# Last batch's rows: plain loads and 0/1 products in place of indexed gathers, and the mean's share added ahead

## The chip, the core and the metric

The kernel runs on one core of a Trainium2 chip. The metric is device time in microseconds, the median of several runs. The core has five engines with a queue of instructions each, worked off in order: PE (TensorE, with its weight loads shown as PEld), DVE (VectorE), ACT (ScalarE), POOL (GpSimd) and SP (SyncE, which here issues transfers and little else). ACT, POOL and SP issue DMA transfers, and 16 DMA engines carry them out. A queue whose head waits holds all that is behind it.

## The reference

Masked attention over 8 batches of 512 features x 1024 tokens, plus the input. One projection serves as queries, keys and values:

```python
q = xt @ Wq.T                       # xt: (B, T, D), 8 heads of 64
scores = scale * jnp.einsum('bhqd,bhkd->bhqk', qh, qh)
logits = (scores * cmask + (1.0 - cmask) * NEG) * rmask
attn = jax.nn.softmax(logits, axis=-1)
ctx = jnp.einsum('bhqk,bhkd->bhqd', attn, qh)
out = ctx @ Wo.T
return x + jnp.transpose(out, (0, 2, 1))
```

The mask has ones for about half of the tokens. A token with mask 0 has all its logits 0, so its attention is the same for every key and its context is the mean of all values: all such tokens of a batch get one and the same output row, called the mean's share here.

## The kernel before

Only the kept tokens (mask 1) go through attention: each batch's are packed into NK = 536 columns (a longer version and a general one follow in the program for inputs that don't fit, and are not run). The packed tokens form NC = 5 chunks, four of 128 and a short one (index 4, LAST) of 24. Eight heads are worked in four pairs per batch. One loop in `late` runs over the 32 pairs and, in each, over five chunks: scores of the chunk (PE), exponentials with their row sums (ACT), and the weighing of values (PE, `av`), with tasks between them. Which task is issued at which (batch, pair, chunk) and in which rank within it stands in a table that `plan` fills with `put`. The position in that table is the position in each engine's queue. `weigh_behind` gives its first matmul a wait on a named instruction, the last one that read the tile it overwrites; for the last chunks that is "partials", the copy of a partial output.

Tiles carry batch and pair or chunk in their names: `pa_7_3` is the partial output of batch 7 (the last), chunk 3. For an ordinary batch the projected rows go to DRAM (`od`), each to the place that `places` gives it, and indexed gathers by POOL (`fetch`, with addition) bring one row per token to `g`, which already holds the input; DVE transposes it (`finish_blocks`) and `store_whole` writes it out, the eight pieces by turns on SP and ACT.

The last batch is different, so that little is left after its last pair. `begin_outputs` multiplies the contexts of pairs 0 to 2 by the output weights during pair 3 and copies the partial sums out of PSUM on ACT (`pa`). After the last chunk come the sums and their inverses (`sum_last`, `inverses`), whose reciprocals PE spreads over partitions (`rb`, L828) and ACT copies (L835), then `end_values_last` (cT), and `end_outputs` adds pair 3's product (`po`) to `pa` on DVE (`oc`, three buffers) and stores the rows to `od_7`. The last packed row holds the mean's share, and tokens with mask 0 point to it. Then `fetch_last` gathers, for each of eight tiles of 128 tokens, the rows named by `origin`, on POOL; `finish_tokens` turns each tile by four PE transposes, DVE adds them to the input in `residual`, and SP and ACT store by turns.

## Time and profile before

| | us |
|---|---|
| runs | 726.7, 728.66, 724.15 (median 726.7) |
| the profiled execution | 730.38 |
| its span | 728.6 |
| PE busy in the span | 642.4 (88%) |
| end of the last weighing's `rb` matmuls (PE) | 694.12 |
| ACT's copy of it (L835) begins | 696.14 |
| `po` begins on PE | 698.18 |
| last rows of `od_7` issued | 706.48 |
| last gather issued on POOL | 715.67 |
| last addition on DVE begins | 722.58 |
| last store issued (ACT) | 723.30 |

The profile's times run from the span's start. A row of the timeline has the start, the length, the engine, the line, the operation with its tiles, and in brackets the idle time before it and what ended that. "ACTq" and "SPq" are those engines' transfer issues. A row of the chain of waits has start, length and what the end waited for at that time. The granted clock is the share of full TensorE speed.

### The profile page before, as it was taken

The page shows a single profiled execution, that of the slowest core. Times are in us where ns is not written, and L with a number is a line of the kernel's source. Part 1 is how long each engine was busy: PE and PEld are TensorE (multiplying, and loading weights), DVE is VectorE, ACT ScalarE, POOL GpSimd, SP SyncE. Part 2 cuts the span into 40 slices and gives each one's busy share as a digit, 9 for nine tenths or more (in the row PEclk, how much of TensorE's full clock was granted, in tenths as well). Part 3 has the DMA queues.
Part 4 walks back from the last instruction along what each step waited for, and adds up shares of the span by engine and source line. Part 5 has one row for each costly group of instructions (what it writes and reads, how often), then busy time and mean ns, then how long its engine had stood idle before and what let it go on. Part 6 is the DMA issues. An engine that isn't in the chain of part 4 may idle for free.

```text
span 728.6 us, 24594 instructions
## 1 busy us (share of the span) xinstructions
PE 642.4 (88%) x10533; PEld 419.8 (58%) x10533; DVE 403.1 (55%) x1137; ACT 322.1 (44%) x874; POOL 208.5 (29%) x228
## 2 busy tenths in 40 slices
PE   6887875899889998899889998899998999998854
PEld 5654453577556675567556675567654677554323
DVE  5578286674564775476664665576531553254333
ACT  4463542555435553356425453255443555445200
POOL 2324204000241403441241402532232411343412
PEclk9999898999999999999999998899998999999975
DMA  8787443253346956778557956665436626769867
GB/s 238 225 259 204 131 121 113 79 153 90 100 129 184 206 125 186 196 196 195 154 162 209 196 134 183 182 167 118 118 93 162 136 64 181 209 140 302 135 179 214
DMA packets 78310, 119.60 MB, mean 164 GB/s; under 512 B 13736, under 2 KB 46976, under 8 KB 78064
## 3 DMA queue, kind: packets, MB, share of 16 engines
q1 hardware_dynamic: 44448, 66.73, 31.2%
q0 software_dynamic: 15936, 35.41, 21.8%
q10 hardware_dynamic: 17808, 15.81, 8.5%
q8 instruction: 84, 1.38, 0.8%
q14 instruction: 34, 0.28, 0.1%
HBM read 74.29 MB, written 42.57 MB: 160 GB/s over the span
## 4 chain that ended last, share of the span: by engine, by line
PE 77%; issue 5%; DVE 5%; ACT 2%; another core or an unknown queue 2%; DMA 1%; ACTq 1%; POOL 0%; POOLq 0%; DVEq 0%
PE av L778 20%; PE s L731 18%; PE pq L590 15%; PE po L906 12%; PE v L369 3%; PE po L981 3%; PE s L745 2%; PE pa L981 2%; PE x L369 1%; PE pq L602 1%; DVE xbar L476 1%; PE x L922 1%; DMA g<-od,origin 1%; DVE len L681 1%
## 5 line engine op out<-in xcount | busy, mean ns | idle before, releaser
L754 ACT ACTIVATE e<-s,bias 128x536 f32<-128x536 f32 x256 | 179.1, 705 | 82.1 <-PE s L731 75.7
L731 PE MATMUL s<-qT 64*64 64x268 f32 x2048 | 179.1, 404 | 17.4 <-issue 15.6
L778 PE MATMUL av<-e,v 64*64 64x268 f32 x2048 | 165.7, 408 | 15.5 <-ACT qT L614 7.5
L731 PEld LDWEIGHTS s<-qT 64*64 64x64 f32 x2048 | 93.5, 138 | 75.2 <-issue 42.5
L590 PE MATMUL pq<-xc,wqT 64*64 64x269 f32 (+1 forms) x896 | 117.9, 397 | 1.1 <-DVE sums L842 0.9
L590 PE MATMUL pq<-xc,crossT 64*64 64x269 f32 (+1 forms) x896 | 113.6, 398 | 0.0
L778 PEld LDWEIGHTS av<-e,v 64*64 64x64 f32 x2048 | 80.6, 139 | 53.4 <-ACT cT L810 11.4
L648 DVE COPY v<-v 128x512 f32<-128x512 f32 x32 | 22.1, 692 | 144.6 <-PE v L369 144.6
L1064 POOL DMA_INDIRECT g<-od,block_origin x56 | 88.8, 1585 | 39.3 <-DMA g<-xd 16.3
L906 PE MATMUL po<-woT,cT 64*64 64x256 f32 x1536 | 98.1, 380 | 1.2 <-issue 1.0
L936 POOL DMA_DIRECT2D od<-oc x28 | 16.9, 603 | 252.0 <-ACT oc L959 226.1
L525 POOL DMA_INDIRECT xin<-xd,source x63 | 61.7, 979 | 92.5 <-DVE source L513 55.8
L906 PEld LDWEIGHTS po<-woT,cT 64*64 64x64 f32 x1536 | 65.1, 134 | 25.2 <-DVE v L663 8.1
L590 PEld LDWEIGHTS pq<-xc,wqT 64*64 64x64 f32 x896 | 66.3, 138 | 18.0 <-DVE sums L842 1.4
L590 PEld LDWEIGHTS pq<-xc,crossT 64*64 64x64 f32 x896 | 65.4, 138 | 15.9 <-issue 0.8
L754 ACT ACTIVATION_READ_ACCUMULATOR e<-s,bias 128x1 f32 x256 | 50.7, 198 | 0.0
L663 DVE COPY v<-x 128x128 f32<-128x128 f32 x32 | 9.2, 289 | 74.9 <-PE x L369 33.0
L810 ACT COPY cT<-av 128x536 f32<-128x536 f32 x31 | 18.8, 606 | 71.6 <-PE av L778 50.1
L614 ACT COPY qT<-pq 128x536 f32<-128x536 f32 x31 | 18.8, 606 | 71.4 <-PE pq L590 30.2
L754 ACT ACTIVATE el<-s,bias 128x268 f32<-128x268 f32 x64 | 30.5, 482 | 44.6 <-PE s L745 44.6
L1038 DVE STREAM_TRANSPOSE whole<-g 128x512 f32<-128x512 f32 x56 | 40.0, 750 | 12.5 <-DMA g<-od,block_origin 12.5
L498 DVE TENSOR_SCALAR_CACHE_REDUCE junk<-rank,place 128x1024 f32<-128x1024 f32 (+4 forms) x35 | 39.1, 1116 | 0.5 <-DMA rank<-ranks 0.5
(186 smaller groups left out, 770.9 us busy)
## 6 DMA issues: line engine op xcount, KB each, us to landing
xd<-xt SPq DMA_DIRECT2D x28, 512.0 KB
g<-xd SPq DMA_DIRECT2D x56, 256.0 KB
x<-in_x_dram SPq DMA_DIRECT2D x40, 256.0 KB
rb<-row SPq DMA_DIRECT2D x60, 160.0 KB
od<-oc POOLq DMA_DIRECT2D x28, 256.0 KB
out_dram<-whole SPq DMA_DIRECT2D x28, 256.0 KB
out_dram<-whole ACTq DMA_DIRECT2D x28, 256.0 KB
x<-in_x_dram ACTq DMA_DIRECT2D x24, 256.0 KB
```

Of the source, the lines that this page charges most:

```text
L369: nc.tensor.matmul(to, block, ident[heads[r], heads[r]], start=True, stop=True)
L498: nc.vector.tensor_scalar(junk[:, : T - at], rank[:, at:], place[:, col], 0.0, ALU.is_le, ALU.add, accum_out=found[:, col])
L525: nc.gpsimd.indirect_dma_start(out=to, out_offset=None, in_=of, in_offset=bass.IndirectOffsetOnAxis(ap=at, axis=0),)
L590: nc.tensor.matmul(pq[heads[c], r, :n], w[heads[r], k // 2, pr * P + c * DK : pr * P + (c + 1) * DK], xcs[b][heads[r], k, :n], start=(k == 0),
L648: copy = nc.vector.tensor_copy(v[:, :LAST, :].rearrange("p c (h d) -> p h c d", h=2), pt[:, :, :E].rearrange("p h (c d) -> p h c d", c=LAST),)
L731: nc.tensor.matmul(s[h][to, hf, :KH], qT[heads[h], at : at + DK], qT[heads[h], hf * KH : (hf + 1) * KH], start=True, stop=True,)
L754: act = nc.scalar.activation(e[:, h], of[h], AF.Exp, bias=biases[pair][:, c : c + 1], scale=SCALE, accum_out=acc[:, h, c : c + 1],)
L778: mm = nc.tensor.matmul(avs[pair][heads[h], hf, :KH], v[rows, c, heads[h]], e[rows, h, hf, :] if c < LAST else e[rows, h, :], start=(c == ...
L906: mm = nc.tensor.matmul(po[heads[c], eb, :E], cTs[b, pr][heads[r], i * P + c * DK : i * P + (c + 1) * DK], woT[heads[r], pr, eb * E : (eb ...
L981: nc.tensor.matmul(po[j * n : (j + 1) * n, :w], cTs[b, pr][:, at : at + n], woT[:, pr, j * w : (j + 1) * w], start=(pr == first), stop=(pr ...
L1038: nc.vector.transpose(in_blocks(wholes[b], b)[:, i].rearrange("p (k h) t -> p k h t", h=2), parted(gs.pop((b, i))),)
L1064: nc.gpsimd.indirect_dma_start(out=gs[b, i], out_offset=None, in_=ods[b], in_offset=bass.IndirectOffsetOnAxis(ap=block_origin[:, b, i : i ...
```

## The change

Six things change, all of them in the last batch except the second half of the fifth.

1. The rows of batch 7 are written in plain rank order, so that those that a tile of 128 tokens needs stand together. `load_begins` reads on SP, from `last_begin`, the row at which each tile starts into registers (seven loads), and `fetch_last` loads 128 rows from there by plain transfers on SP. POOL's eight gathers are gone, as are the load and copy of `origin`. `clear_outputs` zeroes the rows past the kept ones ahead.
2. `finish_tokens` no longer transposes by the identity but multiplies by a 0/1 matrix (`hot_last`) per tile, which puts the row of each kept token to its column and gives the others zero. `place_spots`, `load_spots` and `find_spots` make these matrices in earlier chunks. The PSUM tags of the eight tiles go round three names in place of two.
3. The mean's share is added ahead: `mean_output` projects it (16 short matmuls), DVE copies it, and SP sends it to DRAM and back (`spread_mean`) as rows on all partitions (`mean_wide`) and as a column (`mean_col`). `add_mean` adds the column to the whole `residual`, eight operations on POOL.
4. So the kept tokens must not get it twice: the copy of the partial outputs becomes a subtraction of `mean_wide` on DVE, no longer a copy on ACT.
5. The four short stores of `od_7_4` go to SP in place of ACT. The output stores of batches 6 and on go to SP alone; batch 5 and earlier still alternate.
6. `keep_mean` of the last pair is called in chunk 0, not 1.

On **DVE** at the end of the last pair, before (L1038 are the transposes of batch 6, L842 to L849 the sums and their reciprocals):

```order
L1038 STREAM_TRANSPOSE whole_6_8851<-g_6_4_8637 128x16x32
L1038 STREAM_TRANSPOSE whole_6_8851<-g_6_5_8716 128x16x32
L1038 STREAM_TRANSPOSE whole_6_8851<-g_6_6_8718 128x16x32
L1038 STREAM_TRANSPOSE whole_6_8851<-g_6_7_8763 128x16x32
L842 TENSOR_TENSOR sums_1_88<-sums_1_88,share_7_3_8751 128x10
L845 TENSOR_TENSOR low_85<-low_85,sums_1_88 128x8
L846 TENSOR_SCALAR sums_1_88<-sums_1_88 128x2x4
L848 RECIPROCAL ris_1_90<-sums_1_88 128x2x4
L849 COPY ris_1_90<-sums_1_88 128x2
```

and after, where L1093 are the transposes and L847 to L854 the sums:

```order
L1063 TENSOR_TENSOR pa_7_1_9003<-pa_7_1_8996,mean_wide_8888 128x512
L1063 TENSOR_TENSOR pa_7_2_9005<-pa_7_1_8996,mean_wide_8888 128x512
L1093 STREAM_TRANSPOSE whole_6_8925<-g_6_4_8681 128x16x32
L1093 STREAM_TRANSPOSE whole_6_8925<-g_6_5_8760 128x16x32
L1063 TENSOR_TENSOR pa_7_3_9029<-pa_7_3_9025,mean_wide_8888 128x512
L1093 STREAM_TRANSPOSE whole_6_8925<-g_6_6_8762 128x16x32
L1093 STREAM_TRANSPOSE whole_6_8925<-g_6_7_8807 128x16x32
L847 TENSOR_TENSOR sums_1_90<-sums_1_90,share_7_3_8795 128x10
L850 TENSOR_TENSOR low_87<-low_87,sums_1_90 128x8
L851 TENSOR_SCALAR sums_1_90<-sums_1_90 128x2x4
L853 RECIPROCAL ris_1_92<-sums_1_90 128x2x4
L854 COPY ris_1_92<-sums_1_90 128x2
```

The subtractions stand between the transposes, and the last two transposes and the sums now stand behind that of chunk 3.

On **ACT** at the same place, before (L1008 the copies of partial outputs, L1045 the stores of batch 6):

```order
L1008 COPY pa_7_1_8929<-pa_7_1_8922 128x512
L1008 COPY pa_7_2_8931<-pa_7_1_8922 128x512
L754 ACTIVATE el_7_3_4_8935,sums_1_88<-s_7_3_4_8936,bias_7_3_8749 128x268 x2
L1008 COPY pa_7_3_8955<-pa_7_3_8951 128x512
L1045 DMA out_0_dram<-whole_6_8851 32x8x256 x4
L835 COPY rb_7_3_8980<-rb_3_8981 128x128
L836 COPY rb_7_3_8980<-rb_3_8981 128x512
L936 DMA od_7_9015<-oc_7_0_9013 128x512
L946 DMA od_7_9015<-oc_7_4_9017 24x4x32 x4
```

and after:

```order
L759 ACTIVATE e_7_3_3_8975,sums_1_90<-s_7_3_3_1_8977,bias_7_3_8793 128x536
L759 ACTIVATE el_7_3_4_9009,sums_1_90<-s_7_3_4_9010,bias_7_3_8793 128x268 x2
L840 COPY rb_7_3_9062<-rb_3_9063 128x128
L841 COPY rb_7_3_9062<-rb_3_9063 128x512
L953 DMA od_7_8068<-oc_7_0_9095 128x512
L953 DMA od_7_8068<-oc_7_1_9104 128x512
```

The copies and the stores of batch 6 are gone from ahead of the copy of `rb`.

On **SP** from batch 6's last input rows on, before:

```order
L1032 DMA g_6_7_8763<-xd_6_101 128x512
L1045 DMA out_0_dram<-whole_5_8500 32x8x256 x4
L1045 DMA out_0_dram<-whole_6_8851 32x8x256 x4
L1660 TENSOR_LOAD flag_62
L1660 ISA x2
```

and after (L1032, L1040 and L1047 carry the mean, L1101 are the stores of batches 5 and 6, L963 the short stores of `od_7_4`, L1144 the first of the eight row loads):

```order
L1087 DMA g_6_7_8807<-xd_6_103 128x512
L1101 DMA out_0_dram<-whole_5_8544 32x8x256 x2
L1032 DMA means_of_81<-mean_8864 1x128 x4
L1040 DMA mean_wide_8888<-means_of_81 128x512
L1047 DMA mean_col_8890<-means_of_81 32x4x1 x4
L1101 DMA out_0_dram<-whole_5_8544 32x8x256 x2
L1101 DMA out_0_dram<-whole_6_8925 32x8x256 x8
L963 DMA od_7_8068<-oc_7_4_9098 24x4x32 x4
L1144 DMA g_7_0_9123<-od_7_8068 128x512
L1144 ISA
L1144 DMA g_7_1_9125<-od_7_8068 128x512
```

SP issues the row loads behind eight stores of batch 6 and the short rows.

The diff, cut:

```diff
...
     def keep_mean(pair):
         qms[pair] = sb.tile([P, 1], F32, tag="qm", name="qm_%d_%d" % pair, bufs=4)
         nc.vector.tensor_copy(qms[pair], qTs[pair][:, QW : QW + 1])
+        if pair[0] == B - 1:
+            lasts[pair[1]] = qms[pair]
 
     def project(pair, sweep, read=None):
 
...
 
     def place_outputs(b):
         if b not in ods:
-            ods[b] = dr.tile([NK, D], F32, tag="od", name=f"od_{b}")
+            if b < B - 1:
+                ods[b] = dr.tile([NK, D], F32, tag="od", name=f"od_{b}")
+            else:
+                ods[b] = dr.tile([LP + P + P, D], F32, name=f"od_{b}", bufs=1)
         return ods[b]
+
+    def clear_outputs():
+
+        od = place_outputs(B - 1)
+        nc.gpsimd.dma_start(
+            od[NK:, :].rearrange("(o n) c -> o n c", o=1),
+            seen["zero"].unsqueeze(1).to_broadcast([1, LP + 2 * P - NK, D]),
+        )
 
     def products(po, b, i, sweep, read=None):
 
...
 
     def store_result(b, i, oc, queue):
         od = place_outputs(b)
+        at = places[i] if b < B - 1 else slice(i * P, min((i + 1) * P, NK))
         if i < LAST:
-            queue.dma_start(od[places[i], :], oc)
+            queue.dma_start(od[at, :], oc)
             return
         for j in range(P // SH):
             rows = oc[(j + 1) * SH - END : (j + 1) * SH, :SW]
             if b < B - 1:
-                queue.dma_start(od[places[i], j * SW : (j + 1) * SW], rows)
+                queue.dma_start(od[at, j * SW : (j + 1) * SW], rows)
                 continue
...
             nc.scalar.copy(oc[:, :n], po[:, j, :n])
             store_result(b, i, oc, nc.gpsimd)
 
+    def mean_output(b):
+
+        pt = banks("mean_t")
+        for pr in range(ND):
+            for j in range(P // SH):
+                nc.tensor.matmul(
+                    pt[j * SH : (j + 1) * SH, 0, :SW],
+                    lasts[pr].to_broadcast([P, SH]),
+                    woT[:, pr, j * SW : (j + 1) * SW],
+                    start=(pr == 0),
+                    stop=(pr == ND - 1),
+                )
+        mean = seen["mean"] = keep.tile([P, SW], F32, name="mean")
+        nc.vector.tensor_copy(mean, pt[:, 0, :SW])
+        for j in range(P // SH):
+            nc.sync.dma_start(
+                means_of[j * SW : (j + 1) * SW].rearrange("(o c) -> o c", o=1),
+                mean[j * SH : j * SH + 1, :],
+            )
+
+    def spread_mean():
+
+        wide = seen["mean_wide"] = sb.tile([P, W], F32, tag="rb", name="mean_wide")
+        nc.sync.dma_start(wide[:, :D], means_of.partition_broadcast(P))
+        col = seen["mean_col"] = keep.tile([P, ND], F32, name="mean_col")
+        by = means_of.rearrange("(h d c f) -> c h f d", h=2, c=2, f=Q)
...
+    def add_mean(r):
+        for d in range(ND):
+            part = residual[r][:, d, :NB]
+            nc.gpsimd.tensor_scalar(part, part, seen["mean_col"][:, d : d + 1], None, ALU.add)
+
     def begin_outputs(b, chunks):
 
         po = banks("pa_%d_%d" % (b, chunks[0]))
...
         for j, i in enumerate(chunks):
             n = D if i < LAST else SW
             pa = sb.tile([P, D], F32, tag="xin", name=f"pa_{b}_{i}", bufs=NC)
-            copy = nc.scalar.copy(pa[:, :n], po[:, j, :n])
+            mean = seen["mean_wide"][:, :D] if i < LAST else seen["mean"]
+            copy = nc.vector.tensor_tensor(pa[:, :n], po[:, j, :n], mean, ALU.subtract)
             reads["partials"] = copy.ins.name
             partials[i] = pa
 
...
                     )
                 else:
                     nc.vector.tensor_tensor(oc[:, :SW], po[:, j, :SW], partials[i][:, :SW], ALU.add)
-                store_result(b, i, oc, nc.scalar)
+                store_result(b, i, oc, nc.scalar if i < LAST else nc.sync)
 
         return end
 
...
 
     def store_whole(b, i):
         a, ks = piece(i)
-        (nc.sync, nc.scalar)[i % 2].dma_start(
+        queue = nc.scalar if i % 2 and b < B - 2 else nc.sync
+        queue.dma_start(
             by_quarters(out[b])[a][:, ks, :], wholes[b][a * Q : (a + 1) * Q, ks, :]
         )
+
+    def load_spots():
+
+        wide = seen["spots"] = sb.tile([P, T], F32, tag="rank", name="spots", bufs=1)
+        nc.sync.dma_start(wide, spots_of.partition_broadcast(P))
+
+    def find_spots(first, last):
+
+        if first == 0:
+            seen["hot"] = sb.tile([P, NT, P], F32, tag="junk", name="hot_last", bufs=1)
+        for i in range(first, last):
+            nc.vector.tensor_scalar(
+                seen["hot"][:, i, :],
+                seen["spots"][:, i * P : (i + 1) * P],
+                key[:, 0:1],
+                None,
+                ALU.is_equal,
+            )
+
+    def load_begins():
+
+        seen["begins"] = [
+            nc.values_load(
+                last_begin[0:1, i : i + 1],
+                engines=[mybir.EngineType.SP],
...
+            )
+            for i in range(NT)
+        ]
 
     def fetch_last(b):
 
         for i in range(NT):
             tag, bufs = ("xin", NC) if i < NC else ("g", NT)
             g = sb.tile([P, D], F32, tag=tag, name=f"g_{b}_{i}", bufs=bufs)
-            most = min(NK, END + (i + 1) * P)
-            nc.gpsimd.indirect_dma_start(
-                out=g,
-                out_offset=None,
-                in_=ods[b][0:most, :],
-                in_offset=bass.IndirectOffsetOnAxis(ap=origin[:, i : i + 1], axis=0),
-            )
+            most = (i + 1) * P if i < LAST else LP + 2 * P
+            rows = ods[b][0:most, :]
+            at = seen["begins"][i] if i else 0
+            nc.sync.dma_start(g, rows[bass.ds(at, P), :] if i else rows[:P, :])
             gs[b, i] = g
 
     def fetch(b, i):
...
 
         r, at = divmod(i * P, NB)
         xr = residual[r][:, :, at : at + P]
-        pt = banks(f"o_{b}_{i}", ("t", "av")[i % 2])
+        pt = banks(f"o_{b}_{i}", ("t", "av", "s", "s")[i % 4])
         o = pt[:, 0, :].rearrange("p (d t) -> p d t", d=ND)
         for d in range(ND):
-            nc.tensor.transpose(o[:, d, :], gs[b, i][:, d * P : (d + 1) * P], ident)
+            nc.tensor.matmul(
+                o[:, d, :],
+                gs[b, i][:, d * P : (d + 1) * P],
+                seen["hot"][:, i, :],
+                start=True,
+                stop=True,
+            )
         nc.vector.tensor_tensor(xr, o, xr, ALU.add)
         (nc.sync, nc.scalar)[i % 2].dma_start(
             out[b, :, i * P : (i + 1) * P].rearrange("(d p) t -> p d t", d=ND), xr
...
         nc.vector.tensor_scalar(home, home, float(NK - 1), None, ALU.min)
         nc.sync.dma_start(places_of.rearrange("b (c p) -> (b c) p", p=P), home)
 
+    def place_spots():
+
+        mrow, rank = seen["rowed"], seen["rank"]
+        home, wrap = homes
+        nc.vector.tensor_tensor(wrap[:, 0:1], rank[:, 0:1], mrow[:, 0:1], ALU.subtract)
+        nc.vector.tensor_scalar(home, rank, wrap[:, 0:1], None, ALU.subtract)
+        nc.vector.tensor_tensor(home, home, mrow, ALU.mult)
+        nc.vector.tensor_scalar(home, home, -1.0, None, ALU.add)
+        nc.sync.dma_start(
+            spots_of.rearrange("(c p) -> c p", p=P), home[(B - 1) * NT :, :]
+        )
+
...
         last = B - 1
         put((last, 1, 3), load_residual, 0, rank=8)
         put((last, 2, 3), load_residual, 1, rank=8)
+        put((1, 2, 2), place_spots, rank=20)
+        put((last, 0, 2), load_spots, rank=1)
+        for i in range(2):
+            put((last, 0, 3 + i), find_spots, i * NT // 2, (i + 1) * NT // 2, rank=20)
+        put((last, 0, 1), clear_outputs, rank=2)
+        put((1, 2, 2), load_begins, rank=1)
+        put((last, 3, 0), keep_mean, pairs[-1], rank=0)
+        put((last, 3, 0), mean_output, last, rank=12)
+        put((last, 3, 1), spread_mean, rank=1)
+        for r in range(2):
+            put((last, 3, 4), add_mean, r, rank=31)
         put((last, 3, 2), begin_outputs, last, (0, LAST), rank=11)
         put((last, 3, 3), begin_outputs, last, (1, 2), rank=11)
         put((last, 3, 4), begin_outputs, last, (3,), rank=11)
...
                 if c == 1 and before and not final:
                     load_inverses(before)
                 run(1, 5)
-                if c == 1:
+                if c == 1 and not final:
                     keep_mean(pair)
                 if c == 1 and second:
                     contexts(second)
```

More of the change, by code (lines that the diff above doesn't have):

```diff
@@ L349, in attention_of_kept_tokens @@
     kept = keep.tile([P, B], F32, name="kept")
-    origin = keep.tile([P, NT], I32, name="origin")
+    last_begin = keep.tile([1, NT], I32, name="last_begin")
+    means_of = dr.tile([D], F32, name="means_of", bufs=1)
+    spots_of = dr.tile([T], F32, name="spots_of", bufs=1)
     block_origin = keep.tile([P, B, NT], I32, name="block_origin")
@@ L668, in turn_last_values @@
         return end
+    lasts = {}
     squares = {}
@@ L940, in store_result @@
             if b < B - 1:
-                queue.dma_start(od[places[i], j * SW : (j + 1) * SW], rows)
+                queue.dma_start(od[at, j * SW : (j + 1) * SW], rows)
                 continue
             for h in range(max(1, 2 * SW // D)):
-                g, at = divmod(j * SW // Q + h * KK, KK)
+                g, k = divmod(j * SW // Q + h * KK, KK)
                 n = min(SW // Q, KK)
                 queue.dma_start(
-                    od[places[i], :].rearrange("n (k h f) -> n h k f", h=2, f=Q)[:, g, at : at + n],
+                    od[at, :].rearrange("n (k h f) -> n h k f", h=2, f=Q)[:, g, k : k + n],
                     rows[:, h * HD : h * HD + n * Q].rearrange("n (k f) -> n k f", f=Q),
@@ L998, in whole_output @@
             store_result(b, i, oc, nc.gpsimd)
+    def mean_output(b):
[21 more added lines that the diff above has]
+        by = means_of.rearrange("(h d c f) -> c h f d", h=2, c=2, f=Q)
+        with nc.allow_non_contiguous_dma(reason="features of each partition"):
+            for c in range(2):
+                for h in range(2):
+                    at = c * DK + h * Q
+                    nc.sync.dma_start(col[at : at + Q, :], by[c, h])
+    def add_mean(r):
+        for d in range(ND):
+            part = residual[r][:, d, :NB]
+            nc.gpsimd.tensor_scalar(part, part, seen["mean_col"][:, d : d + 1], None, ALU.add)
     def begin_outputs(b, chunks):
@@ L1044, in store_whole @@
         a, ks = piece(i)
-        (nc.sync, nc.scalar)[i % 2].dma_start(
+        queue = nc.scalar if i % 2 and b < B - 2 else nc.sync
+        queue.dma_start(
             by_quarters(out[b])[a][:, ks, :], wholes[b][a * Q : (a + 1) * Q, ks, :]
         )
+    def load_spots():
[17 more added lines that the diff above has]
+                engines=[mybir.EngineType.SP],
+                min_val=0,
+                max_val=min(i * P, NK),
+                skip_runtime_bounds_check_because="counts of ones in the tokens ahead, and the minimum with the capacity is taken on the chip",
+            )
+            for i in range(NT)
+        ]
     def fetch_last(b):
@@ L1196, in early @@
         nc.tensor.matmul(fits[:, 0:B], spread[:, 0, :], same, start=True, stop=True)
+        ends = pt[:, 0, 2 * P : 2 * P + NT]
+        nc.tensor.matmul(ends, spread[:, 0, :], before[:, B - 1, :], start=True, stop=True)
         nc.tensor.matmul(ranked, upto, mcol, start=True, stop=True)
@@ L1205, in early @@
         nc.vector.tensor_copy(kept, fits[:, 0:B])
+        nc.vector.tensor_scalar(last_begin, ends[0:1, :], float(NK), None, ALU.min)
         nc.vector.tensor_tensor(odd, mrow, isone, ALU.not_equal)
@@ L1352, in place_all @@
         nc.sync.dma_start(places_of.rearrange("b (c p) -> (b c) p", p=P), home)
+    def place_spots():
[8 more added lines that the diff above has]
+        )
     def load_places():
-        placed = sb.tile([P, B + 1, NT], F32, tag="rt", name="placed")
+        placed = sb.tile([P, B, NT], F32, tag="rt", name="placed")
         with nc.allow_non_contiguous_dma(reason="tokens of each partition"):
-            nc.sync.dma_start(placed[:, :B, :], places_of.rearrange("b (p i) -> p b i", i=NT))
-            nc.sync.dma_start(placed[:, B, :], places_of[B - 1].rearrange("(c p) -> p c", p=P))
+            nc.sync.dma_start(placed, places_of.rearrange("b (p i) -> p b i", i=NT))
         seen["placed"] = placed
     def turn_places():
-        nc.vector.tensor_copy(block_origin, seen["placed"][:, :B, :])
-        nc.vector.tensor_copy(origin, seen["placed"][:, B, :])
+        nc.vector.tensor_copy(block_origin, seen["placed"])
     crossed = range(ND + 1, (B - 1) * ND + 1)
```

## The prediction

> **What bounds the kernel now.** I read the page first, then the chain of waits from 655 us on, then the timeline, the groups and the windows of that stretch. The page:
>
> ```profile
> span 728.6 us, 24594 instructions
> PE 642.4 (88%) x10533; PEld 419.8 (58%) x10533; DVE 403.1 (55%) x1137; ACT 322.1 (44%) x874; POOL 208.5 (29%) x228
> ```
>
> TensorE works through nearly the whole span, and the change leaves its main products alone. So the place to look is where PE does not set the pace, the end. The chain there (start, length, what):
>
> ```profile
> 691.19 0.37 ACTq L1045
> 694.17 1.94 ACTq L1045
> 696.14 0.28 ACT rb L835
> 697.66 0.38 DVE cT L818
> 698.18 2.67 PE po L981 x10
> 706.48 2.60 DMA od<-oc
> 715.67 5.65 DMA g<-od,origin
> 721.46 1.10 PE o L1086 x4
> 722.58 0.69 DVE residual L1087
> ```
>
> First ACT cannot copy the inverses (L835), because four output stores of batch 6 (L1045) stand ahead in its queue. Then po (L981) runs. Then the projected rows go to DRAM (od) and come back through GpSimd's gathers (g, L1055), and tiles are turned, added and stored. The timeline gives the lengths:
>
> ```profile
> 668.05 1.08 PE L731 MATMUL s<-qT 64*64 64x268 f32 x16
> 673.96 3.64 PE L981 MATMUL pa<-woT,cT 128*128 128x512 f32 x30
> 680.48 5.42 PE L981 MATMUL pa<-woT,cT 128*128 128x512 f32 x12
> 688.82 0.71 DVE L1038 STREAM_TRANSPOSE whole<-g 128x512 f32<-128x512 f32 x1 [1.08 <-DMA g<-od,block_origin]
> 689.45 0.13 DVE L842 TENSOR_TENSOR sums<-sums,share 128x10 f32<-128x10 f32 x1
> 690.14 0.12 DVE L849 COPY ris<-sums 128x2 f32<-128x2 f32 x1
> 691.11 0.59 ACT L1008 COPY pa<-pa 128x512 f32<-128x512 f32 x1 [3.11 <-PE pa L981]
> 692.81 1.31 PE L828 MATMUL rb<-ident,ris 128*64 128x128 f32 x20
> 698.18 7.28 PE L981 MATMUL po<-woT,cT 128*128 128x512 f32 x16 [4.05 <-DVE cT L818]
> 705.83 1.00 POOL L1055 DMA_INDIRECT g<-od,origin  x1 [21.51 <-DVE oc L1021]
> 709.40 0.95 POOL L1055 DMA_INDIRECT g<-od,origin  x1 [0.30 <-DMA od<-oc]
> 710.34 1.09 PE L1086 MATMUL o<-ident,g 128*128 128x128 f32 x4 [3.18 <-DMA g<-od,origin]
> 715.67 0.95 POOL L1055 DMA_INDIRECT g<-od,origin  x1 [0.30 <-issue]
> 723.30 0.38 ACTq L1088 DMA_DIRECT2D out_dram<-residual  x1
> ```
>
> A product of 512 columns has two records here: six of them took 5.42 us before 698 (0.90 each), while po's four with four short ones took 7.28. The windows say why (busy us of PE, PEld, DVE, ACT, POOL, then the granted clock, the DMA share, GB/s):
>
> ```profile
> 106.40:108.80 2.40, 0.01 (x1) 0.00 (x0) 2.23 (x5) 1.04 (x4) 0.00 (x0) 1.00 0.03 12
> 200.00:201.00 1.00, 1.00 (x36) 0.80 (x36) 0.18 (x1) 0.95 (x4) 0.00 (x0) 0.50 0.00 0
> 655.00:665.00 10.00, 8.69 (x112) 4.57 (x116) 4.15 (x11) 3.80 (x11) 2.69 (x5) 1.00 1.07 356
> 690.50:694.00 3.50, 2.77 (x38) 1.58 (x36) 0.00 (x0) 0.59 (x1) 0.00 (x0) 1.00 0.96 193
> 694.00:698.00 4.00, 0.13 (x4) 0.00 (x0) 1.46 (x6) 0.76 (x2) 0.00 (x0) 0.97 1.05 293
> 698.00:704.50 6.50, 6.32 (x15) 2.40 (x16) 1.42 (x5) 0.00 (x0) 0.00 (x0) 0.50 0.31 83
> 715.50:722.00 6.50, 4.08 (x17) 2.72 (x16) 2.77 (x4) 0.00 (x0) 0.95 (x1) 0.50 1.01 300
> ```
>
> After 4.05 us without work PE got half the clock (0.50) for all of po and most of the tail. From 715.5 the DMA engines are full (share 1.01).
>
> **The change part by part.** All sums are on the profiled execution: 730.38 us with a span of 728.6. The median of the runs shown is 726.7, 3.7 lower; the difference found is taken off the median. More rows that it needs:
>
> ```profile
> L1008 ACT COPY pa<-pa 128x512 f32<-128x512 f32 (+1 forms) x5 | 2.4, 524 | 13.4 <-PE pa L981 13.4
> L1021 DVE TENSOR_TENSOR oc<-po,pa 128x512 f32<-128x512 f32 x4 | 2.6, 686 | 5.1 <-PE po L981 5.1
> L1055 POOL DMA_INDIRECT g<-od,origin x8 | 7.7, 959 | 24.6 <-DVE oc L1021 21.5 <-issue 1.5 <-DVE flag L1596 1.3
> L870 SPq EVENT_SEMAPHORE  x60: 27/28/3467, 53.2 to 650.4; - x60
> L870 SPq DMA_DIRECT2D rb<-row x60: 333/588/1556, 53.3 to 650.9; - x60
> L1204 DVE TENSOR_SCALAR hot<-count,spot x8: 280/281/287, 7.1 to 8.5; 128x128 f32<-128x128 f32 x8
> L1218 DVEq TENSOR_LOAD <-begin x1: 1891/1891/1891, 9.8 to 9.8; - x1
> L450 POOL COPY xr<-xt 128x512 f32<-128x512 f32 x8 | 5.0, 621 | 4.8 <-DMA xd<-xr 3.9 <-ACT qT L572 0.9
> ```
>
> *Mean products.* Sixteen short matmuls stand ahead of scores on PE. The row of x30 is three long ones (2.7 us) and twelve short (0.9), so sixteen cost 1.2 us at most; 0.9 us of it would vanish only if PE were waiting there. I take +1.0.
>
> *Subtracting copies.* pa moves from ACT (0.59 for 512 columns) to DVE (0.69, and about 0.3 for the short one). PE waits for them (the "partials" read), three times: +0.2, +0.3, +0.1, so +0.6.
>
> *DVE's order.* Before, all eight transposes of batch 6 and the sums were done by 690.26, before pa_7_3 ended at 691.70. Now pa_7_3 stands ahead of the last two transposes and the sums. pa_7_3 ends at 691.70 + 1.0 + 0.6 = 693.3; two transposes (2 x 0.71) and the sums chain (689.45 to 690.26, 0.81) bring the inverses to 695.55. The rb matmuls, at 692.81 before, start 2.75 later.
>
> *ACT's queue.* The four stores are gone from it, and nothing stands between rb and its copy: 695.55 + 1.31 = 696.9, against 696.14. The 4.45 us of waiting that go are thus almost eaten by the late inverses. The steps from copy to po took 2.04 us (696.14 to 698.18): po starts at 698.95, +0.8.
>
> *po and the clock.* PE is now idle from 696.86 to 698.95, 2.1 us in place of 4.05. A gap of the same kind (106.4 to 108.8) left the clock at 1.00, so I expect po at full speed, about 3.7 us. But od's stores then come under another limit: oc has three buffers, and oc_7_3 waits until od_7_1 has landed. oc_7_1 is ready at about 701.6, its store lands 2.60 later, 704.3; then 0.69 for oc_7_3 and 2.60 to land: 707.6 without contention. The last two stores of batch 6 run just then, so I take 708.4, 0.7 before the old 709.08.
> The Trainium skill ("TensorE: Matmul & The Clock Gate", section "Part 1: The HAM clock gate") says that the clock is halved after an idle window of about 3.4 us that runs freely; by that a 2.1 us gap leaves po fast, and the sum stands. The trace agrees for the 4.05 us gap; the half clock at 200 us, with PE busy all through, says that this is not the whole condition.
>
> *The tail.* Eight gathers cost 0.96 us each with 0.30 between on POOL; the last was issued 6.6 us after od_7_3 landed. Now SP issues one short store (0.4) and eight loads, about 0.5 each with the register arithmetic (plain issues in the rows take 0.33 to 0.59): the last is issued at 708.4 + 4.4 = 712.8, 2.9 earlier. But in the changed program the transfers of SP and ACT share semaphores, and the short store ahead of the loads waits until od_7_3 is down; so no load starts earlier, while the first gather of before left at 705.83 and PE began its first tile at 710.34. So less than 2.9 is kept. By bytes: eight loads (2.1 MB) and the first three output stores (0.8 MB), which share the engines, take 9.7 to 8.2 us at 300 to 356 GB/s; from about 710, a microsecond after the first load's issue, the last rows land at 718 to 720. I take 719.0 against 721.32 (715.67 + 5.65). The 0/1 products have the form of the transposes and cost the same 1.1 us a tile. From the last rows to the end of the span stay 7.28 us: span 726.3, -2.3.
>
> *Hidden work.* SP's seven register loads (1.9 us where DVE did such), the spots' broadcast, eight comparisons (0.28 each) and five small DVE operations lie where no end waits for them; uncovered they would cost 2.3 us on DVE. Eight additions on POOL (about 0.62 each, 5 us) come after the last gather of batch 6 and end before the first tile needs them. Clearing od is one POOL issue in batch 7's first part. I count 0, bounds 0 to +1.5.
>
> **The sum:** +1.0 +0.6 +1.15 (the rest of the late inverses) -1.95 (ACT free) = +0.8 at po; po's faster clock turns this to -0.7 at od_7_3; the tail makes it -2.3. Prediction: 726.7 - 2.3 = **724.4**.
>
> **The rivals.**
> 1. *The clock falls all the same.* Then po ends 0.8 later than before, od_7_3 lands at 709.9 to 711, and the tail's gain shrinks to 0.8 or nothing: 725.6 to 727.2. For it speaks the row at 200 us. Chance 0.22.
> 2. *The mean comes late (slower).* pa_7_0 needs the broadcast mean, and behind it in DVE's order stand batch 6's transposes, while PE's weighing waits for the same read. The products stand ahead of the scores at 668.05, so the copy is ready at about 669; four issues (1.3 us), a wait of up to 3.47 (the longest of L870's, which is the same round trip) and a flight of 2.60 to 5.65 put it at 676 to 680. Wanted it is at 677.6 + 1.0 = 678.6. Every us past that goes straight to the end; from 680.9 on the kernel is slower than before. It gets there if the two stores of batch 5 ahead of it on SP hold it too, or all its flights are as long as the longest: landing at 684 gives 726.7 + 5.4 - 2.3 = 729.8. Against it: most of L870's waits are 28 ns. Chance 0.13.
> 3. *One queue is slower.* With stores on SP alone the engines were full at 193 GB/s (690.5 to 694), with ACT's beside them at 293. Eight row loads at 193 take 10.9 us: last rows at 722.3, the end 1.0 later: 727.7. It decides below about 2.1 MB in 9 us, 230 GB/s. Against it: 655 to 665, mostly SP's loads, moved 356. The Trainium skill ("DMA: Bandwidth & Descriptors", section "Issuing engines are not separate DMA queues") says that a second issuing engine saves only its issue time; by that this rival has no place, and the two rates above differ by the kind of transfer. Chance 0.08.
> 4. *The tail is shorter still.* Loads at 356 GB/s from 709.6, products at full clock (0.55 a tile), the last store alone on the engines: last rows at 717, the end 5 to 7 us earlier: 719.5 to 721.5. Chance 0.15.
>
> **How the numbers follow.** My forecast (0.42) holds from 722 to 726.5. The range of 718.5 to 730.2 takes in all rivals but the far end of the late mean and of the shorter tail. About 1% (7 us) is what a measurement of this kernel can tell from no change: faster than 719.4 is only the best part of rival 4 and the chance that the tail is worth more than I can see, 0.13; slower than 734 needs a mean that lands after 688, or that together with rival 3, 0.07; the rest, 0.80, is within 1%.
>
> **What would show it.** After: no store of batch 6 on ACT; rb matmuls about 2.7 us later than 692.81, and ACT's copy right behind; po in under 4.5 us at clock 1.00; od_7_3 landing near 708.4; eight row loads issued within 5 us; last rows near 719. Wrong I am if DVE's pa_7_0 waits for a DMA, if PE's clock still drops before po, or if row loads come slower than one in 1.2 us.

## The result, and the profile after

The changed kernel takes 753.2 us against 727.7 for the kernel before: ratio 1.034, 95% interval 1.028 to 1.040. The forecast was 724.4, a time within 1% of the kernel before. Executions over 1.5% slower than the fastest of the same kernel are left out of all ratios. The profiled execution has a span of 749.1 us, 20.5 over the 728.6 of before; the medians differ by 25.5, since the profiled execution of before (730.38) was slower than each of the four timed beside the change, and that of the changed kernel (750.86) one of its faster ones. Its page has the same engines just as busy:

```profile
span 749.1 us, 24781 instructions
PE 646.0 (86%) x10599; PEld 418.6 (56%) x10599; DVE 408.6 (55%) x1155; ACT 319.9 (43%) x869; POOL 213.9 (29%) x229
```

PE is busy 3.6 us longer in a span that is 20.5 us longer, so most of the time is in waits. Where they are is seen by setting the same work side by side (starts in us, from the timelines of both kernels):

| place | before | after | shift |
|---|---|---|---|
| scores of the short chunk, an earlier pair of batch 6 | 581.33 | 579.88 | -1.5 |
| the same, pair 0 of batch 7 | 615.73 | 631.43 | +15.7 |
| the same, pair 2 | 662.43 | 679.37 | +16.9 |
| scores of pair 3, chunk 1 | 668.05 | 686.12 | +18.1 |
| weighing behind pa_7_0 | 679.41 | 698.49 | +19.1 |
| rb on PE | 692.81 | 713.89 | +21.1 |
| po on PE | 698.18 | 717.28 | +19.1 |
| last store of od_7 | 706.48 | 728.55 | +22.1 |
| last addition on DVE | 722.58 | 742.89 | +20.3 |

Some 17 of the 20.5 us arise in one place, more than 100 us before the end, of which the prediction showed no row. In the kernel before, PE comes to the same products of `v` without a wait:

```profile
609.13 0.69 PE L369 MATMUL v<-ident,qT 64*64 64x64 f32 x32
```

The timeline of the changed kernel there:

```profile
600.57 0.66 POOL L910 DMA_DIRECT2D od<-zero  x1
601.78 18.09 SPq L867 DMA_DIRECT2D row<-rt  x4
621.48 0.32 ACTq L1101 DMA_DIRECT2D out_dram<-whole  x1
621.85 0.61 ACT L618 COPY qT<-pq 128x536 f32<-128x536 f32 x1 [15.71 <-DMA row<-rt]
622.60 1.14 PE L371 MATMUL v<-ident,qT 64*64 64x64 f32 x32 [14.83 <-ACT qT L574]
632.24 0.88 DVE L1115 TENSOR_SCALAR hot_last<-spots,key 128x128 f32<-128x128 f32 x4 [7.74 <-DMA spots<-spots_of]
```

and its windows (busy us of PE, PEld, DVE, ACT, POOL, then clock, DMA share, GB/s):

```profile
605.00:610.00 5.00, 2.78 (x52) 1.60 (x44) 0.00 (x0) 1.14 (x4) 0.00 (x0) 1.00 0.94 27
610.00:615.00 5.00, 0.00 (x0) 0.00 (x0) 0.00 (x0) 0.00 (x0) 0.00 (x0) 0.58 0.88 27
615.00:620.00 5.00, 0.00 (x0) 0.00 (x0) 0.00 (x0) 0.00 (x0) 0.00 (x0) 0.50 0.58 25
```

POOL issues the transfer that clears the padding rows of od_7: 232 rows of zeros, 475 KB, all read from one row on one partition. For ten us no engine does anything, while the DMA engines are 58 to 88% busy and move 25 to 27 GB/s. SP's four row stores of 1.2 KB each (L867) take 18.09 us to issue, where the four at the same place of the kernel before took 1.60. Two of the issue instructions are themselves 9.52 and 7.09 us long, and the trace shows no semaphore that they wait for; what holds them inside is not shown. ACT's output store shares a semaphore with one of these stores and waits for its landing; behind it in ACT's queue stands the copy of qT, and PE waits for that 14.83 us. The rest of the 17 us is PE's clock, halved by then: the weighing and the scores behind the wait took 2.01 us each in place of 1.09. In the trace the zeros have all landed 20.1 us after their issue.

The end of the changed kernel, rows of the timeline and of the chain of waits:

```profile
697.55 0.69 DVE L1063 TENSOR_TENSOR pa<-pa,mean_wide 128x512 f32<-128x512 f32 x1 [2.72 <-DMA mean_wide<-means_of]
698.49 1.14 PE L783 MATMUL av<-e,v 64*64 64x268 f32 x16 [1.69 <-DVE pa L1063]
701.20 12.36 POOL L1052 TENSOR_SCALAR residual<-residual,mean_col 128x512 f32<-128x512 f32 x8 [0.28 <-DMA mean_col<-means_of]
712.27 0.44 DVE L847 TENSOR_TENSOR sums<-sums,share 128x10 f32<-128x10 f32 x1
712.95 0.65 DVE L851 TENSOR_SCALAR sums<-sums 128x8 f32<-128x8 f32 x1
713.89 1.31 PE L833 MATMUL rb<-ident,ris 128*64 128x128 f32 x20 [1.57 <-DVE ris L854]
715.25 0.27 ACT L840 COPY rb<-rb 128x128 f32<-128x128 f32 x1 [8.55 <-PE rb L833]
717.28 7.19 PE L998 MATMUL po<-woT,cT 128*128 128x512 f32 x16 [2.08 <-DVE cT L823]
727.83 0.69 DVE L1076 TENSOR_TENSOR oc<-po,pa 128x512 f32<-128x512 f32 x1 [2.88 <-DMA od<-oc]
```

```profile
728.55 2.32 DMA od<-oc
731.24 2.58 DMA g<-od
733.95 8.92 PE o L1170 x64
742.89 0.69 DVE residual L1177
```

ACT's copy now follows rb at once, as forecast, but po still took 7.19 us, oc_7_3 waited 2.88 us for a buffer, and in the tail PE works through all eight tiles without a pause.

### The profile page after: what moved, and what is told of

It reads as the page before. It is cut to its first block, busy times and chain, and to the rows that moved or that the text cites. A ratio compares the mean times of both kernels' runs of the same rounds, so it can differ in the third digit from the quotient of the medians.

```text
span 749.1 us, 24781 instructions
## 1 busy us (share of the span) xinstructions
PE 646.0 (86%) x10599; PEld 418.6 (56%) x10599; DVE 408.6 (55%) x1155; ACT 319.9 (43%) x869; POOL 213.9 (29%) x229
## 4 chain that ended last, share of the span: by engine, by line
PE 74%; DVE 6%; issue 4%; DMA 4%; SPq 3%; ACT 2%; another core or an unknown queue 1%; DVEq 0%
PE av L783 18%; PE s L736 17%; PE pq L594 14%; PE po L922 11%; PE po L998 3%; PE v L371 3%; SPq L867 2%; PE s L750 2%; PE x L371 1%; PE pq L606 1%; PE o L1170 1%; PE pa L998 1%; DVE xbar L478 1%; DMA spots<-spots_of 1%
## 5 line engine op out<-in xcount | busy, mean ns | idle before, releaser
L736 PE MATMUL s<-qT 64*64 64x268 f32 x2048 | 181.5, 403 | 18.6 <-issue 16.6
L594 PE MATMUL pq<-xc,crossT 64*64 64x268 f32 (+1 forms) x896 | 112.5, 395 | 0.0
L652 DVE COPY v<-v 128x512 f32<-128x512 f32 x32 | 22.1, 691 | 158.5 <-PE v L371 158.5
L922 PE MATMUL po<-woT,cT 64*64 64x256 f32 x1536 | 96.5, 379 | 1.6 <-DVE v L667 1.5
L922 PEld LDWEIGHTS po<-woT,cT 64*64 64x64 f32 x1536 | 63.3, 134 | 26.7 <-DVE v L667 9.8
L594 PEld LDWEIGHTS pq<-xc,wqT 64*64 64x64 f32 x896 | 65.1, 137 | 17.6 <-DVE sums L847 1.4
L1093 DVE STREAM_TRANSPOSE whole<-g 128x512 f32<-128x512 f32 x56 | 39.6, 747 | 3.6 <-DMA g<-od,block_origin 3.6
L371 PE MATMUL v<-ident,qT 64*64 64x64 f32 x1024 | 25.0, 242 | 18.7 <-ACT qT L574 18.6
```

What stands on the lines that cost most here:

```text
L371: nc.tensor.matmul(to, block, ident[heads[r], heads[r]], start=True, stop=True)
L594: nc.tensor.matmul(pq[heads[c], r, :n], w[heads[r], k // 2, pr * P + c * DK : pr * P + (c + 1) * DK], xcs[b][heads[r], k, :n], start=(k == 0),
L652: copy = nc.vector.tensor_copy(v[:, :LAST, :].rearrange("p c (h d) -> p h c d", h=2), pt[:, :, :E].rearrange("p h (c d) -> p h c d", c=LAST),)
L736: nc.tensor.matmul(s[h][to, hf, :KH], qT[heads[h], at : at + DK], qT[heads[h], hf * KH : (hf + 1) * KH], start=True, stop=True,)
L922: mm = nc.tensor.matmul(po[heads[c], eb, :E], cTs[b, pr][heads[r], i * P + c * DK : i * P + (c + 1) * DK], woT[heads[r], pr, eb * E : (eb ...
L1093: nc.vector.transpose(in_blocks(wholes[b], b)[:, i].rearrange("p (k h) t -> p k h t", h=2), parted(gs.pop((b, i))),)
```

## The experiments

Ratios are to the kernel before, run on the same chip in turn, with 95% intervals.

### The clear: is it the cause, and does its size set the price?

Edit of the first run:

```diff
-            seen["zero"] = keep.tile([1, D], F32, name="zero")
+            seen["zero"] = keep.tile([P, D], F32, name="zero")
...
+        half = (LP + 2 * P - NK) // 2
         nc.gpsimd.dma_start(
-            od[NK:, :].rearrange("(o n) c -> o n c", o=1),
-            seen["zero"].unsqueeze(1).to_broadcast([1, LP + 2 * P - NK, D]),
+            od[NK:, :].rearrange("(n o) c -> n o c", o=2),
+            seen["zero"][0:half, :].unsqueeze(1).to_broadcast([half, 2, D]),
```

> The changed kernel, with one edit: the zeros that clear the padding rows of od_7 are read from 116 partitions (two rows each) instead of all 232 rows from one partition. Theory A (the one-partition source holds the DMA engines: 475 KB landed after 20.1 us with a DMA share of 0.94 at 27 GB/s, and ACT's and SP's transfers behind it waited): the clear lands in under 6 us, PE's gap of 14.8 us before L371 at 607 to 622 is gone, and the time falls by 15 to 17 us, from 753 to 736 to 738. Rival B (the gap comes from what else was put on SP and ACT there, the spots' broadcast and the register loads, and the clear only runs beside it): 750 or more.

Measured: 740.8 us, 1.019 (1.012 to 1.026). The wait of PE shrinks from 14.83 to 2.00 us, and another one comes to light:

```profile
605.26 0.69 PE L371 MATMUL v<-ident,qT 64*64 64x64 f32 x32 [2.00 <-ACT qT L574]
615.15 0.88 DVE L1116 TENSOR_SCALAR hot_last<-spots,key 128x128 f32<-128x128 f32 x4 [8.43 <-DMA spots<-spots_of]
616.28 3.08 PE L923 MATMUL po<-woT,cT 64*64 64x256 f32 x32 [4.06 <-DVE v L667]
```

Theory A is right on the place, and the amount is less than it said: 1.5% (1.0337 to 1.0188, 10.8 us) went, not 15 to 17 us. The zeros still took 9.8 us to land, not under 6: of the transfer's 16 completion marks in the trace (updates of its semaphore) twelve came 3.3 to 4.7 us after the issue and four only after 9.0 to 9.8. The edit also changes the shape of the transfer (116 times two rows in place of one time 232). Against the rival that the first shape used few of the engines speaks that none of its 16 marks came before 10.8 us and that the share of 0.88 to 0.94 is a mean over all 16 engines. What changed is the time of a packet. Once the stores issued ahead of the clear were done, a 4 KB packet of POOL's queue took 2.3 us (median) with one source partition and 0.16 with 116.

The kernel before, with the clear alone, to an unused DRAM tensor:

```diff
...
+    def clear_scratch():
+        nc.gpsimd.dma_start(
+            scratch.rearrange("(o n) c -> o n c", o=1),
+            seen["zero"].unsqueeze(1).to_broadcast([1, 232, D]),
+        )
...
+        put((last, 0, 1), clear_scratch, rank=2)
```

> The kernel before, with one addition: the same 232 rows of zeros are written from one partition by POOL to an unused DRAM tensor, at the same place in the table (batch 7, pair 0, chunk 1). Theory A: slower by 14 to 17 us, 742 to 745. Rival B: 726 to 730, since nothing else of the change is there.

Measured: 747.6 us, 1.028 (1.020 to 1.035), 19 us over the kernel before in two executions and more than the 14 to 17 expected. Nothing else of the change was in it, and ACT and PE show the same waits:

```profile
627.09 0.60 ACT L615 COPY qT<-pq 128x536 f32<-128x536 f32 x1 [16.62 <-DMA row<-rt]
627.85 1.13 PE L370 MATMUL v<-ident,qT 64*64 64x64 f32 x32 [15.74 <-ACT qT L573]
```

With 116 rows in place of 232:

> As the run before it, with half the rows (116). Theory A, time by bytes: the transfer lands in about 10 us and costs 5 to 8 us, 733 to 736. If such a transfer has a fixed cost whatever its size: as much as with 232 rows. Rival B: no change.

Measured: 733.2 us in the one execution that counts, 4.7 over the kernel before, without an interval; the trace is of the other one (744.2). In it the transfer landed in 11.1 us against 20.1, and PE's wait is 6.77 us:

```profile
619.84 1.13 PE L370 MATMUL v<-ident,qT 64*64 64x64 f32 x32 [6.77 <-ACT qT L573]
```

So the landing goes nearly by bytes, at 21 to 24 KB per us, and some 4.4 us of it are covered by other work with either size (11.1 less 6.77, 20.1 less 15.74); PE waits for the rest. The clear alone makes most of the loss. Rival B falls.

### What is left: the spots, the clear's place, the mean, the sums

The first of these runs leaves the mean's share out altogether, on top of the wide clear (`mean_output`, `spread_mean`, `add_mean` not called, `pa` copied by ACT):

> The changed kernel with the zeros from 116 partitions and without the mean's share: no mean products, no round trip through DRAM, no additions on POOL, and the partial outputs copied by ACT as in the kernel before (so tokens with mask 0 do not get their share: part of the computation is left out). Theory C (beside the clear, the change loses by the mean: pa_7_0 waited for mean_wide until 697.55, 2.1 us of shift; the subtraction ahead of the last transposes on DVE shifts rb by 2 more): 4 to 6 us under the run with zeros from 116 partitions, 731 to 733. Rival D (the mean is hidden, what is lost beyond the clear is lost in the tail): within 1.5 us of it.

Measured: 733.3 us, 1.009 (1.006 to 1.013), 7 us under the wide clear. With both intervals the difference is 0.2 to 1.7%, some 1.5 to 12.5 us: theory C's 4 to 6 lie inside, rival D's 1.5 at the edge. So the mean's products, its wait, the subtraction and the additions on POOL together are not hidden; their single shares are not shown.

Then, with the mean back in and starting from the wide clear, each part was mended in turn, each on top of the one before:

```diff
-        put((last, 0, 2), load_spots, rank=1)
+        put((last - 1, 1, 2), load_spots, rank=1)
```

> The run with zeros from 116 partitions (740.8), with the spots' broadcast moved from batch 7, pair 0, chunk 2 to batch 6, pair 1, chunk 2; the comparisons stay. In its profile DVE sat 8.43 us before the first comparison until the broadcast had landed, and PE 4.06 us behind DVE's copy of values (L667). Theory E (the broadcast, issued two chunks ahead behind SP's other loads, holds DVE and through it PE): 735 to 737, PE's wait before po at that place back under 1 us. Rival F (the DMA engines were full there, another transfer would be late instead): 739 to 741.

Measured: 735.0 us, 1.010 (1.006 to 1.015). Another 0.8% went, just as much as both intervals together allow by chance; PE's wait at that place is gone from the rows.

```diff
-        put((last, 0, 1), clear_outputs, rank=2)
+        put((1, 2, 3), clear_outputs, rank=2)
```

> The run before it, with the clear (116 partitions) moved from batch 7, pair 0, chunk 1 to batch 1, pair 2, chunk 3, where the DMA share is under 0.5. In the profile with zeros from 116 partitions the clear still took 9.81 us to land, and ACT waited 2.89 us for small row transfers of SP. Theory A: another 2 to 3 us less, 732 to 735. Rival: the wait is moved to batch 1, no gain (within 1 us).

Measured: 734.5 us, 1.011 (1.002 to 1.020): no gain; the rival holds, within the interval.

```diff
-        put((last, 3, 0), keep_mean, pairs[-1], rank=0)
-        put((last, 3, 0), mean_output, last, rank=12)
-        put((last, 3, 1), spread_mean, rank=1)
+        put((last, 2, 3), keep_mean, pairs[-1], rank=0)
+        put((last, 2, 3), mean_output, last, rank=12)
+        put((last, 2, 4), spread_mean, rank=1)
```

> The run before it, with the mean's products and their round trip one pair earlier (batch 7, pair 2, chunks 3 and 4, in place of pair 3, chunks 0 and 1). Theory C (pa_7_0 waits for the round trip: 2.8 us of PE's time in the profile with zeros from 116 partitions, and the products stand on the chain): 3 to 5 us less, 728 to 731. Rival G (the loss there is the subtraction's place in DVE's queue, ahead of transposes and sums, not the wait): 0 to 1 us less.

Measured: 733.6 us, 1.008 (1.003 to 1.013). A change of 0.3%, inside the intervals, which rule out neither C's 3 to 5 us nor rival G's 0 to 1.

```diff
-                put(at, finish_blocks, b, i, rank=22)
+                put(at, finish_blocks, b, i, rank=10 if b == B - 2 and i > 5 else 22)
...
-            nc.gpsimd.tensor_scalar(part, part, seen["mean_col"][:, d : d + 1], None, ALU.add)
+            nc.scalar.add(part, part, seen["mean_col"][:, d : d + 1])
```

> The run before it, with two edits: the last two transposes of batch 6 stand ahead of pa_7_3 in DVE's queue again, and the eight additions of the mean to the residual run on ACT, not on POOL (there they took 1.54 us each, and DVE's small operations beside them 0.44 and 0.65 in place of 0.13 and 0.17). Theory G: rb starts 2 us earlier, stores of batch 6 start earlier and are out of the way of od_7: 2 to 4 us less, 725 to 728. Rival: ACT's additions hold the copy of rb, no gain.

Measured: 729.9 us, 1.004 (1.000 to 1.009). With POOL idle, DVE's small operations have about their old lengths (0.16 and 0.17 in place of the 0.44 and 0.65 of the changed kernel), and rb no longer waits. They had these lengths in the run before it too, where POOL's additions had ended 1.4 us ahead of them, so of this step's 0.3% the lengths explain nothing. The rows:

```profile
692.15 0.69 DVE L1064 TENSOR_TENSOR pa<-pa,mean_wide 128x512 f32<-128x512 f32 x1 [1.67 <-PE pa L999]
692.76 0.16 DVE L847 TENSOR_TENSOR sums<-sums,share 128x10 f32<-128x10 f32 x1
693.15 0.17 DVE L851 TENSOR_SCALAR sums<-sums 128x8 f32<-128x8 f32 x1
```

The four steps together take the kernel from 1.019 back to about that of before, and no further. Whether the two losses, the clear's and the spots', overlap in the changed kernel was tried directly, with the clear left as it was and only the spots moved:

> The changed kernel with one edit, the spots' broadcast moved to batch 6, pair 1, chunk 2, and the clear from one partition left as it is. With the clear widened the same move gave 0.8% (1.0188 to 1.0104). Theory L (the clear's stall gives the broadcast time to land, so the two losses overlap: in the changed kernel's profile PE waits only 1.25 us at L667, against 4.06 with the wide clear): 0 to 3 us less than the changed kernel, ratio 1.030 to 1.034. If the losses simply add up: 6 us less, 1.025.

Measured: 750.3 us, 1.028 (1.024 to 1.031). Against 1.034 that is 0.6%, near the 0.8% with the wide clear, but with both intervals anything from nothing to 1.3%. Theory L's bound of 1.030 and the plain sum of 1.025 both lie inside the interval, so the run does not decide between them. What the rows show speaks for L: in the changed kernel PE waited 1.25 us for DVE's copy of values, against 4.06 with the wide clear.

### The tail

Four short stores moved off SP (`nc.sync` to `nc.gpsimd` for `od_7_4`), on top of the last of the four:

> The run with the sums ahead (729.9), with the four short stores of od_7_4 issued by POOL in place of SP, so that nothing on SP waits for od_7_3 ahead of the row loads. In that run's profile the first load was issued at 708.44, 0.02 us after od_7_3 had landed, while od_7_0 had been down since 701.89. Theory H (the loads wait for od_7_3 only through the short stores ahead of them and the semaphores they share): the first loads leave 1 to 3 us before od_7_3 lands, the time falls by 1 to 2 us, to 728 to 729. Rival I (the tail is set by PE, which worked without a pause at half the clock on the 0/1 products): 0 to 0.5 us.

Measured: 730.5 us, 1.003 (0.999 to 1.006), not told apart from 1.004. In the trace three loads did leave ahead of od_7_3's landing (708.94, 712.56 and 713.32, against 716.41), more than theory H asked for, and the end did not follow. Then eight products that nobody reads, to keep PE's clock:

```diff
+    def keep_busy(tag, n):
+        pt = banks("idle_%d" % n, tag)
+        for k in range(n):
+            nc.tensor.matmul(pt[:, 0, :D], ident, woT[:, 0, :], start=True, stop=True)
...
+        keep_busy("s", 2)
         sum_last(last)
         end_values_last(last)
...
+        keep_busy("av", 6)
         worst = sb.tile([P, 2], F32, tag="worst", name="worst")
```

> The run before it with eight products of 512 columns that nobody reads: two between rb and po, six after po. Theory I (PE's clock: halved after a gap of 2.08 us before po, in every run of this study but one, and again before the tail): po takes 3.7 us in place of 5.9 to 7.2, the tail's products 6.9 us in place of 8.9 to 10, and the time falls by 3 to 5 us, to 724 to 726, under the kernel before. If transfers set the tail: less than 1.5 us.

Measured: 729.2 us, 1.002 (0.997 to 1.006). The clock stayed at 1.00 from po to the end, po took 4.22 us, and still nothing came of it:

```profile
700.56 4.22 PE L999 MATMUL po<-woT,cT 128*128 128x512 f32 x16 [0.17 <-DVE cT L823]
713.36 2.16 PE L1171 MATMUL o<-hot_last,g 128*128 128x128 f32 x16 [1.01 <-DMA g<-od]
717.94 2.93 PE L1171 MATMUL o<-hot_last,g 128*128 128x128 f32 x24 [0.60 <-DMA g<-od]
```

```profile
718.00:720.00 2.00, 2.00 (x18) 2.00 (x19) 0.76 (x2) 0.00 (x0) 0.00 (x0) 1.00 1.12 349
720.00:722.00 2.00, 0.87 (x8) 0.68 (x7) 1.39 (x2) 0.00 (x0) 0.00 (x0) 1.00 1.13 338
```

PE now waits for row loads again, and the DMA engines are full at 338 to 349 GB/s. So the rows speak against theory I: with PE's clock mended, transfers set the pace of the tail. The times alone do not exclude it, since against the run before the gain is 0.1% with up to 0.7% inside the intervals. The same eight products in the kernel before:

> The kernel before with the same eight products that nobody reads. Theory I: po takes 3.7 us in place of 7.3 there too, but oc's three buffers and the gathers' 1.25 us each stay: 2 to 3 us less, 725 to 726. If the gathers on POOL alone set the tail: 0 to 1 us.

Measured: 727.3 us, 1.003 (0.999 to 1.007): no gain there either. Here the clock fell all the same, a little later: po took 5.92 us after a gap of 1.99.

### One part of the change alone

```diff
-        (nc.sync, nc.scalar)[i % 2].dma_start(
+        queue = nc.scalar if i % 2 and b < B - 2 else nc.sync
+        queue.dma_start(
             by_quarters(out[b])[a][:, ks, :], wholes[b][a * Q : (a + 1) * Q, ks, :]
```

> The kernel before with one part of the change alone: batch 6's output stores all on SP, none on ACT. In its profile ACT stood 4.45 us before the copy of rb, of which 2.0 us lay on the chain (rb's products ended at 694.12, the copy began at 696.14). Theory J (the prediction's step: ACT free brings po 2 us forward, and the rest follows): 1 to 2 us less, ratio 0.997 to 0.999. Rival K (the end waits for transfers: stores of batch 6 land later on one queue and meet od_7's): no change or up to 2 us more.

Measured: 725.9 against 729.0 us, 0.995 (0.993 to 0.998): faster than both kernels, the only run here that is. The rows show the step as the prediction had it:

```profile
695.09 1.31 PE L828 MATMUL rb<-ident,ris 128*64 128x128 f32 x20
696.45 0.27 ACT L835 COPY rb<-rb 128x128 f32<-128x128 f32 x1 [2.48 <-PE rb L828]
698.49 5.72 PE L981 MATMUL po<-woT,cT 128*128 128x512 f32 x16 [2.08 <-DVE cT L818]
```

From rb to po it is 3.40 us, 5.37 before. Theory J holds for the step; the gain of 0.2 to 0.7% reaches beyond its 1 to 2 us, and whether something else in the run adds to it is not shown.

## Why the prediction was wrong

**The step that failed** is "Hidden work", with its sentence on the clear: one POOL issue, counted at 0, bounds 0 to +1.5. I priced its issue and not its transfer. In its place the runs showed a transfer that holds SP's row stores, through them ACT's queue and through that PE for 14.83 us. It cost 1.5% to 2.8% of the kernel (10.8 us by widening its source, 19 to 20 as an addition to the kernel before), and the range could not hold that. No rival had it. The source was there to be read in the diff: `to_broadcast([1, ...])` of a tile with one partition. The Trainium skill ("SBUF — State Buffer", section "Door 1: The DMA port swizzle") gives about 27 GB/s for a transfer that reaches one port of SBUF; the trace agrees, with 25 to 27 GB/s in the windows of the result. By that figure the 475 KB take some 17.6 us, an estimate from that page, against the 20.1 measured.

**The spots' broadcast** stood in the same paragraph as work for which no end waits. Its landing was waited for: by DVE's comparisons, which stand ahead of DVE's copy of values in its queue (PE 4.06 us in the run with the wide clear). The move gave 0.6 to 0.8%, 4 to 6 us, in two runs of which neither is clear of its interval alone. The paragraph named a price for DVE's own time (2.3 us) and none for a DVE that waits.

**The mean** (rival 2, chance 0.13): mean_wide landed at 697.43, which is 680.5 when the 16.9 us of earlier shift are taken off, at the end of the 676 to 680 given. Its price was 1.0 us of waiting on top of 1.1 for the products, which were forecast at 1.0. Two of the prediction's signs of being wrong did appear, DVE's pa_7_0 waiting for a transfer and PE's clock dropping before po, but neither carries the loss. Leaving the whole mean out gave 7 us, more than these 2.1; with an interval that starts at 1.5 us, that the rest costs more is not shown.

**The subtracting copies** were forecast at 0.2, 0.3 and 0.1 us more of PE's waiting. The second and third came so: 0.84 and 0.85 us in place of 0.60 and 0.73. The first holds the wait for the mean.

**DVE's order**: rb was forecast 2.75 later; it came 4.2 later (21.1 less 16.9): about those 2.75, the wait for the mean, and 0.8 that was not foreseen: the sums chain took 1.6 us in place of 0.81 while POOL's additions ran beside it. Those took 1.54 us each; the row used for them (0.62) was a copy.

**ACT's queue**: forecast -1.95, measured 19.1 - 21.1 = -2.0, and alone it makes the kernel faster. This term was right.

**po and the clock**: wrong. After a gap of 2.08 us po took 7.19 us in the changed kernel, so rival 1's condition (chance 0.22) came true, and od_7_3 was issued 3.0 us later than po's shift explains (22.1 less 19.1). In other runs with the same gap po took 4.22 to 7.1 us. The Trainium skill ("TensorE: Matmul & The Clock Gate", section "Part 1: The HAM clock gate") has a window that runs freely, which fits that it varies; that a gap shorter than a whole window of about 3.4 us is safe, as I took from it, these rows do not bear out.

**The tail**: from od_7_3's landing (728.55 + 2.32 = 730.87) to the end of the span it was 18.2 us, 19.5 before; forecast 17.9. The sum was nearly right, in part by luck, since its reasons were half wrong. The 0/1 products do not cost what the transposes cost: 64 records for eight tiles where the transposes had 32, and PE became the bound of that stretch at half clock:

```profile
734.00:737.00 3.00, 3.00 (x14) 3.00 (x15) 0.69 (x1) 0.00 (x0) 0.00 (x0) 0.50 0.96 300
737.00:740.00 3.00, 3.00 (x28) 3.00 (x27) 2.06 (x3) 0.00 (x0) 0.00 (x0) 0.98 1.05 357
```

Fourteen records in 3 us are 1.7 us a tile at 0.50, twenty-eight 0.86 at 0.98; the transposes took 1.09 at 0.50.

**One queue** (rival 3) did not happen: the row loads, on SP alone, moved 300 GB/s from 734 to 737 (the 357 after that has output stores of ACT in it). So the 193 GB/s of before is not the rate of one queue. SP's stores there all came from the lower 64 partitions and ACT's from the upper, by `piece(i)` with even and odd i; when SP alone sends both kinds by turns, it moves 285 in the kernel before with one queue (694 to 698), and 294 to 300 in the run with the sums ahead:

```profile
693.00:694.00 1.00, 1.00 (x18) 0.45 (x18) 0.53 (x4) 0.30 (x1) 0.00 (x0) 1.00 1.00 294
694.00:695.00 1.00, 1.00 (x23) 1.00 (x20) 0.00 (x0) 0.00 (x0) 0.00 (x0) 1.00 1.00 300
```

That the half of the partitions makes the 193 is argued from this; no run varies it alone.

**What stays open**: of the last 0.4% between the mended kernel and the kernel before, and of the 0.3% each of the mean's move and of the sums' order, none is clear of its interval. Why the clear in its old place still cost ACT 2.9 us of waiting with a wide source, and yet its move gave nothing, was not settled.

## What to carry to other kernels

Price a transfer that a change adds by its source and destination partitions and its bytes, not by its issue, and then ask which small transfers share its engines and which compute queues wait for those. "Hidden" holds for an engine's busy time only: an instruction that waits for a transfer holds all that stands behind it in its queue, wherever in the program that is. Of a change of six parts, try the parts alone: a half of one of them was worth 0.5%, and one transfer of another cost 2.8% when it was added alone.

## What was not expected of the hardware

- One source partition was read at 25 to 27 GB/s, while the 16 engines showed a share of 0.58 to 0.94: 475 KB took 20.1 us, half of it 11.1, and small transfers of other queues landed only with it (SP's row stores up to 19 us after their issue).
- Spread over 116 partitions the same zeros, issued by POOL, still needed 9.6 to 10.1 us in the eight runs that did so, though twelve of the 16 completion marks came within 5.
- POOL's addition of a column to 128x512 took 1.54 us, its copy of the same size 0.62; beside it DVE's operations on 10 and 8 columns took 0.44 and 0.65 us in place of 0.13 to 0.17.
- A gap of 2.08 us before po left the clock at 1.00 for all of po in one run (4.22 us, the one with the spots early) and halved it in others (up to 7.19 us).
